# Attention measured in another order, an expert schedule with earlier lists, and the two arms of a branch swapped

## The chip, the core and the metric

The kernel runs on one core of a Trainium2 chip. A core has five engines with instruction streams of their own: PE (matmul), DVE (vector), ACT (scalar and activation functions), POOL (general, and here the issuer of gathers and scatters), and SP (issues plain DMAs). They work in parallel and wait for one another on semaphores. Data lies in the DRAM of the chip (HBM), in SBUF (128 partitions), and in PSUM (eight banks of 128 by 512 float32 values), into which PE writes. The metric is the time of one execution on the device in microseconds (us); lower is better. A profile is one execution; its span runs from the first instruction to the last, and the time of the execution is a little more.

## The reference

A layer of a Flamingo model: attention from tokens to a context, with a gate, and then a mixture of eight experts with a gate. There are 8 batches of 512 tokens, 256 channels, 16 heads of 16 channels, and all is float32.

```python
x = x + tanh(g_xattn[0]) * xattn(layernorm(x), ctx, ctx, mask, wq, bq, wk, bk, wv, bv, wo, bo)
x = x + tanh(g_ffn[0]) * ffn(layernorm(x), router_w, router_b, expert_up, expert_down)

def xattn(query, key, value, mask, ...):
    q, k, v = query @ wq.T + bq, key @ wk.T + bk, value @ wv.T + bv      # in 16 heads
    scores = einsum('bhqd,bhkd->bhqk', q, k) / sqrt(16)
    scores = where(mask == 0, -1e9, scores)
    return (softmax(scores) @ v) @ wo.T + bo

def ffn(x, ...):
    probs = softmax(x @ router_w + router_b)
    top_w, top_idx = top_k(probs, 2)
    comb = sum(top_w * one_hot(top_idx, 8))
    return sum(comb[:, e] * (gelu(x @ expert_up[e].T) @ expert_down[e].T) for e in range(8))
```

`expert_up[e]` is 1024 by 256 and `expert_down[e]` 256 by 1024. The mask is 1 by 1 by 512 by 512 and the same for all batches and heads; it is 0 for a prefix of the keys and 1 for the rest, so that at most 128 keys, those at the end, are attended.

## The kernel before

**Two arms.** A prologue loads the mask and finds whether the attended keys lie within one window of 128. The answer is `near_i`, which every engine loads into a register (L1519). `tc.If` (L1522) then takes one of two arms: `attend_near`, written for a window of 128 keys, or `attend_anywhere` with the experts behind it, for any mask. With these inputs `attend_near` runs. Both are in the program, about as long as each other; in this kernel `attend_near` stands first, so an engine that starts it goes straight on and one that ends it jumps over the other arm.

**Prologue.** It computes for batch 0 the layernorm, the queries (`q_ps`), and from a window of the context the keys and values (`kv_ps`), then takes the mask's column out of the window by a matmul with `pick` (`k_ps`). `idle_ps` are matmuls without use that keep PE active.

**Layernorms.** `measure` gives three steps: `look` (four pairs of BATCH_NORM_STATS2 and AGGREGATE on DVE, L225 and L228), `settle` (thirteen small DVE operations, L233 to L246, that make the reciprocal root of the variance and the shift), and the scaling (`scale`, L275: four ACT operations, xn = x times rstd plus shift). `turn` then transposes xn on PE (`xnT_ps`) and copies it on ACT (L286). The letter a marks the norm ahead of the attention, f the one ahead of the experts. `settle` of two norms can go together.

**The attention's loop.** For b from -1 to 7 there are four groups g (which half c of the channels and which half i of its heads) of three slots n. In a slot the hand-written part comes first: `weigh` (`n_av`, weights times values) for the group before, `find_tops` (scores `t_ps` on PE, their maximum over keys by `tops` on DVE, L1033) for the group that follows, `lower_tops` (`top_ps`, a transpose, and `ql`, the queries with their maximum). `weights_T` makes the group's scores again with the maximum subtracted (`w_ps`, PE L1058), exponentiates them on ACT (`n_pT`, L1063). `raw`, `inv`, `n_o`, `oT` on DVE divide the weighted sums. Then come the steps that `between` put into `plan[g, n]` for other batches: the projection of the batch just finished (`proj_ps`, with the add `x` on DVE, L1102), its norm f, router logits (`logits`: `route_ps` on PE, `lgT` on ACT), routing (`route`, below), the places of its tokens in the experts' lists (`place`: `place_ps` on PE, `counts` on ACT), their entry into a table in DRAM (`enter`: scatters by POOL, L398), and for coming batches the norm a, `queries`, `keys_values` (`kv_ps`), `keys_T` (`k_ps` and ACT's four copies `k`, L551 and L557) and `keys_less` (`km`).

`route` (L330) transposes the logits into PSUM (`lg_ps`), adds the router's bias (`lg`), and takes softmax and the two largest with their indices on DVE (L338 to L360), with one Exp on ACT (L341).

**Order.** The tile framework schedules instructions and may move them within an engine's stream. `tc.keep_in_program_order(ins)` pins an instruction, that is, those pinned keep their order on the engine. Of each pair of scalings in `scale` only the first is pinned.

**Experts.** The tokens of one expert come in jobs of up to three tiles of 128. 32 jobs (`MAIN`) always run, more only if needed. A job s has the steps `list_rows(s)` (SP reads a register and copies the table's lines of this job into SBUF as `listed`, L806), `fetch(s)` (POOL gathers the tokens' rows into `xg` by `listed`, L826), `load(s)` (SP loads the expert's `up` and `down`, 1 MB each), `turn_rows(s)` (`xT`), `ups` (`h_ps` on PE, Gelu on ACT, L874 and L878), `fetch_y` (POOL gathers the output so far), `downs` (`o_ps` on PE, `y` on DVE, L892 and L895, and POOL's scatter into `out`, L898). The dictionary `amid` puts the first four jobs (`DONE`) into the attention's loop at (b, g). The rest run in `compute`, which lists job s + 4 and loads job s + 2 while it runs job s. A copy from the table waits for the entries made before it in the program. The norm, routing and places of the last two batches are interleaved into these jobs, one step of `queue` after each step of `compute`.

Of the kernel before, what the change touches and what calls it, by code (L numbers as in the profile page):

```python
# [16 lines left out]
ALU = mybir.AluOpType  # L17
AX = mybir.AxisListType
# [50 lines left out]
def flamingo_layer(ctx: ExitStack, tc: tile.TileContext, a: dict, out: bass.AP):  # L69
# [190 lines left out]
    def shared(p2, small, bank):  # L260
        def layernorms(jobs, pin=False, measured=None):


            said, looks, settle_all = measured or measure(small, [job[:2] for job in jobs], pin)
            settle = lambda pin=False: settle_all(pin)

            def own(k):
                b, which, dst = jobs[k]

                def scale(ts):  # L270
                    if ts[0] == 0:
                        said[k] = p2.tile([P, QT, D], F32, tag="xn", name=f"xn_{which}_{b}")
                    for t in ts:
                        at = k * QT + t
                        ins = nc.scalar.activation(  # L275
                            said[k][:, t, :], xs[b][:, t, :], AF.Identity,
                            bias=said["shift"][:, at : at + 1], scale=said["rstd"][:, at : at + 1],
                        )
                        if t == ts[0] and pin:
                            tc.keep_in_program_order(ins)  # L280

                def turn(c):
                    ps = bank(f"xnT_ps_{which}_{b}_{c}")
                    for t in range(QT):
                        nc.tensor.transpose(ps[:, t * P : (t + 1) * P], said[k][:, t, c * P : (c + 1) * P], ident)
                    nc.scalar.copy((dst() if callable(dst) else dst)[:, c, :], ps)  # L286

                return (
                    lambda: said[k], [lambda ts=ts: scale(ts) for ts in ((0, 1), (2, 3))],
                    [lambda c=c: turn(c) for c in range(DC)],  # L290
                )

            return looks, settle, [own(k) for k in range(len(jobs))]
# [7 lines left out]
        def finish(b):  # L301
# [28 lines left out]
            def route():  # L330
                ps = bank(f"lg_ps{b}")[:, :P]
                nc.tensor.transpose(ps, said["lgT"], ident)
                lg = t3("lg")
                nc.vector.tensor_tensor(
                    lg, ps.rearrange("p (t e) -> p t e", t=QT)[:, :, :E], over_t(rb), ALU.add
                )
                mx = t2("mx")
                nc.vector.tensor_reduce(mx, lg, AX.X, ALU.max)  # L338
                nc.vector.tensor_tensor(lg, lg, over_e(mx), ALU.subtract)
# [64 lines left out]
            places = [place] + [lambda t=t: enter(t) for t in range(b * QT, (b + 1) * QT)]  # L404
            return x2T, keep_x, keep_rows, logits, route, places

# [42 lines left out]
    with early, tc.tile_pool(name="ps_mask", bufs=1, space=PSUM) as ps_mask:  # L449
# [23 lines left out]

        norms_0 = measure(const, [(0, "a")], True)
        settle_0 = norms_0[2]
# [39 lines left out]
        win = load_window(mk, 0)  # L515
        load_x(1, pin=True)
        wins = {1: load_window(const, 1, pin=True)}
# [90 lines left out]
        nc.vector.scalar_tensor_tensor(near, uneven, 0.0, near, ALU.is_le, ALU.mult)  # L608
        tc.keep_in_program_order(nc.vector.tensor_copy(near_i, near))
        drop = column("drop", P)  # L610
        tc.keep_in_program_order(nc.vector.tensor_scalar(drop, row_ps, -1.0, 1.0, ALU.mult, ALU.add))
# [8 lines left out]

        keep_ones(vals[0])
        for t in vals[1:]:
            keep_ones(t)
# [5 lines left out]
    def experts(pool, seen, half_bank, bank, row_bank):  # L629
# [283 lines left out]

        def compute(s, end, first):

# [13 lines left out]
            else:  # L929

                steps += up[:2] + last + up[2:]
            if s + 4 < end:
                steps.append(lambda: list_rows(s + 4))
# [34 lines left out]
    def attend_near(att):  # L968
# [136 lines left out]

        def normalize(*jobs):
            looks, settle, each = layernorms(jobs, True)
            for job, own in zip(jobs, each):
                normal[job[:2]] = own
            return looks, settle  # L1110

        def between(old, new, next_):
# [9 lines left out]
            if old is not None:  # L1122
                x2T, keep_x, keep_rows, logits, route, place = finish(old)
                jobs.append((old, "f", x2T))
# [5 lines left out]
            if new is not None:  # L1130
# [4 lines left out]
                if new == 1:  # L1135
                    put(1, 1, *turns)
                    put(2, 1, keys_T)
                    put(3, 1, queries[0])
                    put(3, 2, queries[1], keys_less)
                else:  # L1140
                    put(1, 1, *turns, keys_T)
                    put(3, 0, keys_less)
                    put(2, 0, queries[0])
                    put(2, 1, queries[1])
# [6 lines left out]
            if next_ is not None:  # L1151
                put(*((2, 2) if old is None else (0, 2)), looks[-1])
            if old is not None:
# [4 lines left out]
            if jobs:  # L1158
                put(*((3, 1) if old is None else (1, 2)), settle)
            if old is not None:  # L1160
# [5 lines left out]
                counts = [count for count, end in zip(plans, PARTS) if old + 1 == end]  # L1166
                later.append((route, place, enter, counts))
            return plan


        def begin():
# [21 lines left out]
            (7, 3): [lambda: list_rows(5), lambda: fetch(5)] + downs(3)  # L1193
            + [lambda: load(5), lambda: turn_rows(4), lambda: list_rows(6), lambda: list_rows(7)],
        }
        DONE = 4


        xnT, later = {}, deque()
        looks, settle = normalize((1, "a", lambda: xnT[1]))  # L1200
        for step in (*looks, settle):
            step()
        behind = None
        for b in range(-1, B):
# [10 lines left out]
            if b == 0:  # L1215
                plan[0, 0] += looks
                plan[0, 1].insert(0, settle)
            for route, place, enter, counts in behind_route:
                plan[0, 2].append(route)
                plan[1, 2].append(place)  # L1220
# [26 lines left out]
        wait = lambda: None  # L1247
        (route, place, enter, _), (route_last, last, enter_last, counts) = later
        mixed = [step for pair in zip(rest, [route, place, *enter] + [wait] * len(rest)) for step in pair]
        spread = [step for one in enter_last for step in (one, wait, wait)]  # L1250
        queue = deque([*mixed, route_last, last, *spread, *counts])
        for s in range(DONE, MAIN):
            for step in compute(s, MAIN, DONE):
                step()
# [9 lines left out]
    def attend_anywhere(att):  # L1264
# [143 lines left out]
        def end(b):  # L1408
            x2T, keep_x, keep_rows, logits, route, place = finish(b)
            (look,), settle, ((normal, scales, turns),) = layernorms([(b, "f", x2T)])  # L1410
            return [keep_x, look, settle, *scales, lambda: keep_rows(normal()), *turns, logits, route, *place]

# [108 lines left out]
    )  # L1521
    with tc.If(is_near == 1) as which, ExitStack() as att:  # L1522
        attend_near(att)
    with which.Else():
        with ExitStack() as att:
            attend_anywhere(att)
        with ExitStack() as exp:
# [16 lines left out]
            for s in range(MAIN):  # L1544
                for step in compute(s, MAIN, 0):
                    step()
            compute_extra()


# [41 lines left out]
```

## Time and profile before

| what | value |
| --- | --- |
| median of 6 runs | 813.78 us (812.47 to 815.03) |
| time of the profiled execution | 813.25 us |
| its span | 811.5 us |
| mean granted PE clock | 0.968 of full |
| `h_ps` (L874), 1,024 matmuls | 242.9 us |
| `o_ps` (L892), 1,088 matmuls | 243.4 us |
| POOL's three indirect transfers of the experts (L898, L826 twice) | 199.4 us |
| HBM read, written | 92.66 MB, 20.28 MB |

The two groups of expert matmuls make up 60% of the span. The page cuts the span into 40 slices of about 20.3 us; each digit is a share in tenths:

```
PE   8999988888989989999899999999999999999992
DVE  7876885859674664533163353525343433423300
PEclk9997998989899998999999999999999999999997
DMA  5700211000473230143738566666644754654310
```

The first half is the attention, in which DVE is almost as busy as PE; from slice 21 on the experts are alone. Waits of PE by what they were for, from the summary of waits (total, times, longest):

```
PE o_ps L892 <- DVE y L895: 4.2, 4, 1.2
PE lg_ps L332 <- DVE x L1102: 4.1, 4, 1.7
PE x_ps L849 <- DVE raw L1082: 4.1, 2, 3.6
PE route_ps L323 <- ACT x2T L286: 3.6, 1, 3.6
PE xnT_ps_a L285 <- DVE x L1102: 3.5, 3, 1.2
```

At the end the last scatter into `out` is issued at 797.03 us, POOL waits for its landing until 801.7, and the span ends at 811.5 us with the engines' drains.

### The profile page before, as it was taken

Reading aid. Unit: us, or ns where it says so; the run is one execution under the profiler, and the core shown is the slowest. Engines: PE = TensorE matmul, PEld = TensorE weight load, DVE = VectorE, ACT = ScalarE, POOL = GpSimd, SP = SyncE. Lnnn points to the kernel's source line nnn. Section 1 sums busy time; section 2 is a strip of 40 time slices with the busy share of each in tenths; the row PEclk is TensorE's granted clock in tenths of the full one; section 3 lists DMA queues with packets and bytes.
Section 4 is the critical chain, followed back from the end, with each engine's and each line's share of the span. In section 5 each row is a group of like instructions: output and inputs, shape, how many; then the busy total and the mean of one; then the engine's idle time right before and its main releaser. Section 6 shows DMA issues by size and latency. Waiting matters only on the chain. (4 is left out here: it accounts for less than half of the span.)

```text
span 811.5 us, 11155 instructions
## 1 busy us (share of the span) xinstructions
PE 754.4 (93%) x3898; PEld 542.4 (67%) x3898; DVE 409.7 (50%) x1315; ACT 254.7 (31%) x487; POOL 311.5 (38%) x420
## 2 busy tenths in 40 slices
PE   8999988888989989999899999999999999999992
PEld 3444443434465746767688888888788788888871
DVE  7876885859674664533163353525343433423300
ACT  4564745354544434243312111111211211121110
POOL 2021115152637261536563534444443443334330
PEclk9997998989899998999999999999999999999997
DMA  5700211000473230143738566666644754654310
GB/s 163 265 7 8 78 34 56 27 30 27 164 284 116 93 114 20 54 152 106 242 117 308 188 225 205 207 221 201 234 162 152 240 180 153 200 213 163 98 53 24
DMA packets 82728, 113.32 MB, mean 140 GB/s; under 512 B 16605, under 2 KB 67552, under 8 KB 82656
## 3 DMA queue, kind: packets, MB, share of 16 engines
q1 hardware_dynamic: 70000, 85.16, 31.3%
q0 software_dynamic: 11840, 26.76, 10.0%
q8 instruction: 35, 0.57, 0.3%
q10 hardware_dynamic: 816, 0.53, 0.2%
q14 instruction: 37, 0.30, 0.1%
HBM read 92.66 MB, written 20.28 MB: 139 GB/s over the span
## 5 line engine op out<-in xcount | busy, mean ns | idle before, releaser
L892 PE MATMUL o_ps<-down,hT 128*128 128x256 f32 x1088 | 243.4, 381 | 4.2 <-DVE y L895 4.2
L874 PE MATMUL h_ps<-xT,up 128*128 128x256 f32 (+1 forms) x1024 | 242.9, 393 | 3.4 <-DVE xT L851 2.0
L892 PEld LDWEIGHTS o_ps<-down,hT 128*128 128x128 f32 x1088 | 206.1, 191 | 40.5 <-DVE y L895 6.0
L874 PEld LDWEIGHTS h_ps<-xT,up 128*128 128x128 f32 x1024 | 193.2, 190 | 46.4 <-issue 5.4
L863 DVE STREAM_TRANSPOSE xT<-xg 32x128 f32<-32x128 f32 (+1 forms) x368 | 115.7, 314 | 179.7 <-DMA xg<-rows,listed 175.0
L878 ACT ACTIVATE hT<-h_ps 128x512 f32<-128x512 f32 (+1 forms) x144 | 82.1, 573 | 345.8 <-PE h_ps L874 308.7
L898 POOL DMA_INDIRECT out<-y,listed x68 | 68.4, 1006 | 148.4 <-DVE y L895 127.6
L826 POOL DMA_INDIRECT y<-out,listed x68 | 64.9, 955 | 77.1 <-DMA out<-y,listed 48.0
L1033 DVE TENSOR_REDUCE tops<-t_ps 128x4 f32<-128x512 f32 x128 | 79.5, 681 | 24.2 <-PE t_ps L1028 17.5
L1063 ACT ACTIVATE n_pT<-w_ps 128x512 f32<-128x512 f32 x128 | 67.8, 597 | 49.5 <-PE w_ps L1058 45.0
L826 POOL DMA_INDIRECT xg<-rows,listed x68 | 66.1, 972 | 37.6 <-issue 18.9
L398 POOL DMA_INDIRECT table<-entries,place_i x64 | 62.8, 981 | 25.3 <-issue 16.5
L895 DVE SCALAR_TENSOR_TENSOR y<-o_ps,listed,y 128x256 f32<-128x256 f32 x68 | 31.2, 481 | 74.7 <-PE o_ps L892 51.4
L1058 PE MATMUL w_ps<-ql,km 32*128 32x512 f32 x256 | 54.3, 695 | 1.8 <-DVE tops L1033 1.5
L1010 POOL TENSOR_TENSOR x<-x,bo 128x1024 f32<-128x1024 f32 x8 | 18.8, 2354 | 73.1 <-DVE bo L1009 42.3
L1028 PE MATMUL t_ps<-k,q 32*128 32x256 f32 x512 | 44.9, 423 | 1.3 <-ACT n_pT L1063 0.9
L1082 DVE STREAM_TRANSPOSE raw<-n_av 128x512 f32<-128x512 f32 x32 | 22.8, 712 | 42.7 <-PE n_av L1076 23.1
L1028 PEld LDWEIGHTS t_ps<-k,q 32*128 32x128 f32 x512 | 27.6, 194 | 22.8 <-issue 9.7
L1076 PE MATMUL n_av<-n_pT,nv 128*32 128x512 f32 x256 | 38.1, 670 | 1.2 <-DVE xT L851 1.1
L570 PE MATMUL q_ps<-n_xnT,wqT 128*128 128x512 f32 x64 | 31.4, 615 | 0.9 <-ACT n_xnT L286 0.6
L1097 PE MATMUL proj_ps<-woT,oT 128*128 128x256 f32 x128 | 31.5, 388 | 0.0
L1097 PEld LDWEIGHTS proj_ps<-woT,oT 128*128 128x128 f32 x128 | 23.4, 190 | 8.8 <-DVE mv_f_a L228 2.5
(220 smaller groups left out, 529.9 us busy)
## 6 DMA issues: line engine op xcount, KB each, us to landing
up<-in_upT SPq DMA_DIRECT2D x32, 1024.0 KB
down<-in_downT SPq DMA_DIRECT2D x32, 1024.0 KB
out<-x SPq DMA_DIRECT2D x8, 512.0 KB
rows<-xn_f SPq DMA_DIRECT2D x8, 512.0 KB
x<-in_x SPq DMA_DIRECT2D x7, 512.0 KB
table<-none SPq DMA_DIRECT2D x1, 2400.0 KB
xg<-rows,listed POOLq DMA_INDIRECT x68
y<-out,listed POOLq DMA_INDIRECT x68
```

The lines of the kernel that those rows point to most:

```text
L398: nc.gpsimd.indirect_dma_start(out=table_parts[2 * t + i][:, :], out_offset=bass.IndirectOffsetOnAxis(ap=place_i[:, t, i : i + 1], axis=0) ...
L826: ins = nc.gpsimd.indirect_dma_start(out=dst, out_offset=None, in_=src[: seen[JOBS[s][0]], :], in_offset=bass.IndirectOffsetOnAxis(ap=list ...
L863: nc.vector.transpose(dst[32 * g : 32 * g + 32, i], src[32 * i : 32 * i + 32, g])
L874: nc.tensor.matmul(ps[:, i, :], lhsT=up[:, dc, (f + i) * P : (f + i + 1) * P], rhs=xT[:, dc, :], start=(dc == 0), stop=(dc == DC - 1),)
L878: nc.scalar.activation(made[s][:, f : f + m, :], ps, AF.Gelu)
L892: nc.tensor.matmul(ps, lhsT=hT[:, f, h * P : (h + 1) * P], rhs=down[:, f, :], start=(f == 0), stop=(f == FC - 1))
L898: ins = nc.gpsimd.indirect_dma_start(out=out_parts[h][:, :], out_offset=bass.IndirectOffsetOnAxis(ap=listed[:, n, h, 0:1], axis=0), in_=y[ ...
L1028: ins = nc.tensor.matmul(ps[j][:, u], lhsT=q[rows_j, c, t * P : (t + 1) * P], rhs=k[rows_j, c], start=True, stop=True)
L1033: nc.vector.tensor_reduce(top[:, 2 * tp : 2 * tp + 2, :].rearrange("p t (i x) -> p t i x", i=2)[:, :, :, 32 * j], ps[j], AX.X, ALU.max,)
L1058: ins = nc.tensor.matmul(ps[j], lhsT=km[rows_j, c, i, :], rhs=lowered[b, c][rows_j, i, :], start=True, stop=True)
L1063: nc.scalar.activation(pT[:, j, :], ps[j], AF.Exp)
L1097: nc.tensor.matmul(ps[:, t - ts[0], :], lhsT=outs[b, c][:, t * P : (t + 1) * P], rhs=w["woT"][:, c, :], start=(c == 0), stop=(c == DC - 1),)
```

## The change

It has these parts:

1. In `scale` all four ACT operations are pinned.
2. `route` is cut in two. `route` now only transposes and adds the bias, and stands at (0, 0) of the next batch's plan. `choose` does the rest and stands at (0, 2), where all of it stood; its first DVE operation is pinned.
3. Batch 1's x is loaded ahead of batch 0's window on SP, and its `look` and `settle` run in the prologue on DVE, ahead of the branch, into tiles of the constant pool; inside `attend_near` they are gone.
4. In the pass b = 0, in which no older batch is to be finished, batch 3's `look` goes from (2, 2) to (1, 2) and its `settle` from (3, 1) to (2, 0).
5. `keys_T` goes from (1, 1) to (1, 2). There it stands directly ahead of the `place` of the finished batch, with which it shares a PSUM bank.
6. Jobs 6 to 16 (up to `LISTED`) are all listed in one step at (7, 3); `compute` lists from job 17 on.
7. The arms are swapped: `attend_anywhere` is first in the program, `attend_near` last. An engine now jumps over the other arm as it starts `attend_near`, and has nothing to jump over at its end.
8. In the tail's queue `route` and `choose` of one batch are one step.

```diff
@@ def scale
-                        if t == ts[0] and pin:
+                        if pin:
                             tc.keep_in_program_order(ins)
@@ def finish
             def route():
                 ps = bank(f"lg_ps{b}")[:, :P]
                 nc.tensor.transpose(ps, said["lgT"], ident)
-                lg = t3("lg")
+                said["lg"] = t3("lg")
                 nc.vector.tensor_tensor(
-                    lg, ps.rearrange("p (t e) -> p t e", t=QT)[:, :, :E], over_t(rb), ALU.add
+                    said["lg"], ps.rearrange("p (t e) -> p t e", t=QT)[:, :, :E], over_t(rb), ALU.add
                 )
+
+            def choose():
+                lg = said["lg"]
                 mx = t2("mx")
-                nc.vector.tensor_reduce(mx, lg, AX.X, ALU.max)
+                tc.keep_in_program_order(nc.vector.tensor_reduce(mx, lg, AX.X, ALU.max))
...
@@ prologue
-        norms_0 = measure(const, [(0, "a")], True)
+        load_x(1, pin=True)
+        norms_0, norms_1 = (measure(const, [(b, "a")], True) for b in range(2))
...
         win = load_window(mk, 0)
-        load_x(1, pin=True)
...
         tc.keep_in_program_order(nc.vector.tensor_copy(near_i, near))
+        norms_1[1][0]()
...
         keep_ones(vals[0])
+        norms_1[2](True)
@@ def compute
-            if s + 4 < end:
+            if listed <= s + 4 < end:
                 steps.append(lambda: list_rows(s + 4))
@@ def between
-                    put(1, 1, *turns, keys_T)
+                    put(1, 1, *turns)
+                    put(1, 2, keys_T)
...
-                put(*((2, 2) if old is None else (0, 2)), looks[-1])
+                put(*((1, 2) if old is None else (0, 2)), looks[-1])
...
-                put(*((3, 1) if old is None else (1, 2)), settle)
+                put(*((2, 0) if old is None else (1, 2)), settle)
@@ amid
-            + [lambda: load(5), lambda: turn_rows(4), lambda: list_rows(6), lambda: list_rows(7)],
+            + [lambda: load(5), lambda: turn_rows(4), lambda: [list_rows(s) for s in range(6, LISTED)]],
         }
         DONE = 4
+        LISTED = SIZES[0] + SIZES[1]
@@ the attention's loop
-            for route, place, enter, counts in behind_route:
-                plan[0, 2].append(route)
+            for route, choose, place, enter, counts in behind_route:
+                plan[0, 0].append(route)
+                plan[0, 2].append(choose)
                 plan[1, 2].append(place)
@@ the tail's queue
+        def choice(route, choose):
+            route()
+            choose()
+
+        first = [lambda: choice(route, choose), place, *enter]
+        mixed = [step for pair in zip(rest, first + [wait] * len(rest)) for step in pair]
...
-        queue = deque([*mixed, route_last, last, *spread, *counts])
+        queue = deque([*mixed, lambda: choice(route_last, choose_last), last, *spread, *counts])
@@ the branch
-    with tc.If(is_near == 1) as which, ExitStack() as att:
-        attend_near(att)
-    with which.Else():
+
+    with tc.If(is_near == 0) as which:
         with ExitStack() as att:
             attend_anywhere(att)
...
+    with which.Else(), ExitStack() as att:
+        attend_near(att)
```

## The prediction

> **What bounds the kernel now.** I read the page first, then windows by stage, then the timelines of the stages that stood out. The page:
>
> ```profile
> span 811.5 us, 11155 instructions
> ...
> PE 754.4 (93%) x3898; PEld 542.4 (67%) x3898; DVE 409.7 (50%) x1315; ACT 254.7 (31%) x487; POOL 311.5 (38%) x420
> ...
> L1033 DVE TENSOR_REDUCE tops<-t_ps 128x4 f32<-128x512 f32 x128 | 79.5, 681 | 24.2 <-PE t_ps L1028 17.5
> ```
>
> PE (the matmul engine) is busy 93% of the span, so only its idle time and the time that it runs at half clock can be won. The windows say where they are (columns: stretch, length, each engine's busy time and count, granted clock, DMA share, GB/s):
>
> ```profile
> 60.00:76.00 16.00, 14.54 (x62) 6.57 (x62) 9.84 (x30) 7.02 (x15) 2.34 (x1) 0.68 0.03 10
> 100.00:210.00 110.00, 92.94 (x592) 45.08 (x588) 83.30 (x270) 56.55 (x120) 36.76 (x69) 0.93 0.12 37
> 430.00:797.00 367.00, 362.07 (x1609) 304.92 (x1607) 135.75 (x407) 62.25 (x110) 153.51 (x157) 1.00 0.56 187
> ```
>
> From 430 us on the experts run at full clock with 5 us idle: nothing to win. In 100 to 210 PE idles 17 us and loses clock; in 60 to 76 the clock is 0.68. PE there:
>
> ```profile
> 62.35 1.12 PE L1058 MATMUL w_ps<-ql,km 32*128 32x512 f32 x2
> 64.93 3.26 PE L1058 MATMUL w_ps<-ql,km 32*128 32x512 f32 x6 [1.46 <-DVE tops L1033]
> 68.12 1.93 PE L1076 MATMUL n_av<-n_pT,nv 128*32 128x512 f32 x8
> 69.99 3.78 PE L539 MATMUL kv_ps<-wkv,win 128*128 128x512 f32 x4
> 73.70 1.38 PE L1028 MATMUL t_ps<-k,q 32*128 32x256 f32 x16
> ```
>
> Six w_ps take 3.26 us where eight take 1.14 at 108.33; kv_ps takes 3.78 where 1.98 is usual (38.38). PE stopped for tops, and the clock halved. Tops was late because DVE measured batch 3 (st_a at 58.71 to shift_a, raw at 62.75: 4.04 us) with t_ps already done at 61.84.
>
> **The change, part by part.** The sum is made against the profiled run's own 813.25 us (811.5 span, 1.75 around it); the median of six, 813.78, lies 0.53 above it, which I add at the end.
>
> *Batch 3 measured sooner.* The 4.04 us move to before raw at 52.66. DVE idles 1.35 there and 0.69 at 54.9, so 2.04 are covered and 2.0 delay tops and w_ps of that group. In return the stall at 62.35 falls away: at the usual paces w_ps, n_av, kv_ps, t_ps take 1.07 + 1.0 + 1.9 + 1.1 and end at 67.4 instead of 75.08, 7.6 sooner. 7.6 − 2.0 = **−5.6**. Other bound: if the displaced 2.0 us stop PE and halve its clock for one spell of 6.83 us (3.4 lost), 5.4 of 5.6 are given back: 0. I take −5.6, since 2.0 us is less idle than what halved the clock at 131 to 134 (below).
>
> *Batch 1 measured in the prologue.* Its loads are issued on SP ahead of the window's, some 7 us sooner. Its look falls into a DVE idle of 1.51 us at 15.8; its settle (2.5 us) comes after the first keep_ones. DVE thus reaches the branch near 21.1 instead of 18.3, while at present the settle stands behind the branch and holds the first tops to 24.23. Same work in another place: 0 apart from the jump. The earlier load is 512 KB, 1.4 us at the 365 GB/s of that stretch; on SP it now stands ahead of the two window loads, the gates and the small constants, but the DMA engines are idle from 9.8 to 14, so it is off the queue before the windows are issued (12.87): 0, at worst +1.4 if it slows the mask, whose last quarter DVE reads at 8.7.
>
> *The arms swapped.* At the start each engine now takes a jump over the other arm, and at the end none. What a taken jump costs shows at the end of the present program:
>
> ```profile
> L1522 PEldq COMPARE_BRANCH  x1: 90/90/90, 20.1 to 20.1; - x1
> ...
> L959 PEldq COMPARE_BRANCH  x2: 3821/4201/4581, 793.0 to 797.2; - x2
> ...
> L1587 POOLq DRAIN  x3: 40/107/4734, 806.0 to 811.3; - x3
> ...
> L1587 DVEq DRAIN  x2: 10/38/65, 802.1 to 811.0; - x2
> ```
>
> Not taken 0.09 us, taken 3.8 to 4.6 on PE. POOL, last at the end, branches at 803.22 and drains from 805.96: 2.74 us on the path, then 4.73 of drain. **−2.7**; bounded by 0 if the drain ends by something else. At the start PE branches at 20.12; with 4.2 its first t_ps comes at 24.3 instead of 21.83, the first tops about 24.7. DVE took 4.3 from its branch (797.83) to its drain (802.13): from 21.1 that is 25.4. ACT, 2.4 by its own end, reaches its scalings (24.40) 0.4 late. DVE is the bound from 24.23 to 35.85 (four rounds of tops, each 2.48), so its own delay is what counts: 0.5 to 1.2, taken **+1.1**; upper bound +3.5, if PE's 2.5 us of waiting halves its clock.
>
> The Trainium skill bears on this with two places that disagree. Advanced Engine Details and Errata, Control Flow Timing, gives a compare-and-branch about 108 ns; the row of 3,821 to 4,581 ns is some forty times that, so by the page both jumps would be worth an estimated 0.1 us and the sum would lose both terms. Runtime: NRT & Kernel Launch, Instruction fetch mechanics, says that a taken branch out of the fetched window must wait for a new page; that fits the row, and speaks against this change, as the wait is only moved to the start.
>
> *Route split, scalings pinned, keys_T later.* In each of five passes (b = 2 to 6; here b = 2) PE waits thus:
>
> ```profile
> 108.07 0.33 PE L332 MATMUL lg_ps<-ident,lgT 128*128 128x128 f32 x1 [0.80 <-DVE x L1102]
> 115.23 0.66 PE L285 MATMUL xnT_ps_a<-ident,xn_a 128*128 128x128 f32 x4 [1.18 <-DVE x L1102]
> 118.06 0.38 PE L368 MATMUL place_ps<-both,before 128*128 128x32 f32 x2 [0.84 <-ACT k L557]
> ```
>
> lg_ps moves two slots ahead, where its bank is free: −0.8. place_ps now stands directly behind k_ps in one PSUM bank and waits for ACT's four copies of k (1.51 us): about +0.85, with w_ps and n_av queued behind it. But DVE is busy without a break from 104.93 to 124.55, and its x add still releases xnT_ps_a, so PE gains nothing by coming sooner, and most of place's wait fits into the slack ahead of the next tops. Pinned scalings take three ACT operations of 0.52 from ahead of n_pT to another place, worth the 0.45 that t_ps waits at 123.72. I take **0** for the passes; bounds five times −0.8 and +0.85: −4.0 to +4.3.
>
> *Lists 6 to 16 at (7, 3), queue of the tail.* Today a list waits on SP for table entries of batches 6 and 7 that it does not read, and the loads behind it wait too. In 360 to 430:
>
> ```profile
> L874 PE MATMUL h_ps<-xT,up 128*128 128x256 f32 x152 | 35.2, 383 | 3.4 <-DVE xT L851 2.0 <-DMA up<-in_upT 1.4
> ```
>
> All 3.4 is the upper gain, 0 the lower: nine more lists then stand ahead of load 6 on SP, 3 KB each, while PE has other jobs. I take **−2.0**: the wait for up, and a third of that for xT. Route and choose of batches 6 and 7 in one step reorder PE work that the experts' matmuls surround: 0. Where choose's Exp falls between Gelus in batches 6 and 7, ACT reloads its table (1,283 ns each, L878 and L341 there); ACT is idle 34.5 us ahead of its Gelus in that stretch, which hides it, and uncovered it would be 1.3 to 2.6.
>
> Sum: +1.1 − 5.6 + 0 − 2.0 − 2.7 = −9.2. 813.25 − 9.2 = 804.05, and with 0.53 the median: **804.6**.
>
> **The rivals.** *Slower: place_ps halves the clock in each pass.* At 131.37 and 133.02 PE idled 1.22 + 1.70 = 2.92 us within 3.4, and the clock halved at 135.67 for 6.83 us. At 114 to 118 it idled 1.18 + 0.23 + 0.84 = 2.25 and the clock held. With 0.85 more that is 3.1: past the mark, if it lies close enough. Price per pass 0.85 + 3.4 = 4.25. From three of five passes on the rest is outweighed: 12.75 − 9.2 = +3.55, **817.3**; with all five 825. For it: the two idles above, and three spells (135, 173, 207) already within 110 us. Against: the three waits stretch over 4.6 us, and DVE sets the pass, so PE slack absorbs the 0.85.
>
> The page TensorE: Matmul & The Clock Gate, Part 1, has the clock judged in free-running windows of about 3.4 us and only full or half; the spells here, 6.83 and 10.24 us long, are whole multiples of 3.41 and agree. By it 3.1 us over 4.6 would not always fill a window.
>
> *The stall only moves.* Batch 3's measuring stops PE at 55 instead (0 for that term), the start costs 2.5, lists hide nothing, the end gives 2.7: 813.25 − 0.2 + 0.53 = **813.6**. For it: DVE had only 2.04 idle there. Against: tops at 55.60 would be late by 2.0, not by 4.
>
> *Part of the change does not do what it says.* The drain of POOL ends when it did, and the lists were not what held up and xT: −2.7 and −2.0 are lost, 804.6 + 4.7 = **809.3**.
>
> **How the numbers follow.** Forecast 0.50, partial effect 0.16, moved stall 0.12, slower by the clock 0.22. 0.2% is 1.6 us, about what a measurement of this kernel can tell from no change. The moved stall gives 0.03 to faster, 0.06 to same and 0.03 to slower: faster 0.69, same 0.06, slower 0.25. The forecast's own range is 800 to 808 (half of the passes' −4.0, and the start's +3.5 or a lesser gain at 60). For 8 in 10 I go from 799 to 816: it takes in the partial and the moved case, and leaves out most of the slower one.
>
> **What would show it.** Right: w_ps, n_av and kv_ps near 60 to 68 at 1.1, 1.0 and 2.0 us and a clock of 1.00 there; PE's first t_ps near 24.3; POOL's drain straight behind its semaphore work, with no 2.7 between; h_ps in the stretch from 360 to 430 with under 1.5 us of waits; place_ps waiting 1.7 on k, with tops no later. Wrong: clock spells at place_ps, a spell at 55, first tops past 27, or a spell of DVE and ACT lateness such as the 4.04 us at 134.93 in new places, for which this trace shows no cause.

## The result, and the profile after

The changed kernel takes 816.38 us (median of 41 runs), the kernel before 813.41 us (83 runs): a ratio of 1.0025, interval 1.0015 to 1.0035. By the ratio it is slower by about 2 us (the medians lie 3.0 apart); 804.6, with a range to 816, was predicted. The profiled execution took 815.19 us with a span of 813.4. The windows of the changed kernel, in the stretches shown of before (columns as there: stretch, length, busy time and count of PE, PEld, DVE, ACT, POOL, granted clock, DMA share, GB/s):

```profile
60.00:76.00 16.00, 16.00 (x100) 7.43 (x100) 13.12 (x25) 8.60 (x18) 4.46 (x2) 1.00 0.03 10
100.00:210.00 110.00, 92.62 (x594) 47.09 (x596) 81.98 (x270) 55.62 (x116) 37.19 (x70) 0.89 0.10 32
210.00:430.00 220.00, 195.48 (x1128) 141.17 (x1120) 105.74 (x380) 87.30 (x152) 104.62 (x161) 0.95 0.43 141
430.00:797.00 367.00, 361.33 (x1604) 303.98 (x1604) 138.55 (x416) 63.44 (x112) 153.99 (x158) 1.00 0.55 184
```

At 60 to 76 the stall is gone and the clock stays full, as forecast. From 100 to 430 PE idles more than before. When the same matmul starts in the two profiles, read from the two timelines, shows where the time comes and goes:

| point | before, us | after, us | difference | change of it |
| --- | --- | --- | --- | --- |
| first `w_ps` | 37.31 | 40.52 | +3.2 | +3.2 |
| sixth group of `w_ps` | 77.37 | 74.45 | -2.9 | -6.1 |
| last group of `w_ps` | 343.21 | 343.20 | 0.0 | +2.9 |
| 193rd `h_ps` | 388.65 | 385.82 | -2.8 | -2.8 |
| 289th `h_ps` | 438.63 | 444.27 | +5.6 | +8.5 |
| 993rd `h_ps` | 768.48 | 775.17 | +6.7 | +1.1 |
| end of the span | 811.54 | 813.42 | +1.9 | -4.8 |

The 193rd, 289th and 993rd `h_ps` are the first of jobs 6, 9 and 31. The +3.2 at the first `w_ps` is more than one effect: with the arms in their old order (a run below) the changed kernel has it at 36.47, so the swapped arms cost 4.0 there, and the other parts, batch 1 in the prologue first of all, give 0.8 back.

The start, from the instructions of the branch's line and PE's timeline of the changed kernel (in the first line: durations in ns, first and last start):

```profile
L1535 PEldq COMPARE_BRANCH  x1: 4197/4197/4197, 19.9 to 19.9; - x1
```

```profile
24.25 1.94 PE L1033 MATMUL t_ps<-k,q 32*128 32x256 f32 x16 [2.99 <-issue]
26.12 2.84 PE L542 MATMUL kv_ps<-wkv,win 128*128 128x512 f32 x4
```

PE jumps for 4.2 us, idles 2.99 of them, and then runs at half clock: kv_ps takes 2.84 instead of 1.98. The stall near 62 has gone and kv_ps and t_ps have their usual lengths; only the eight w_ps ahead of them take 2.97, where 1.1 was expected:

```profile
65.20 2.97 PE L1063 MATMUL w_ps<-ql,km 32*128 32x512 f32 x8
...
69.10 1.98 PE L542 MATMUL kv_ps<-wkv,win 128*128 128x512 f32 x4
71.02 1.15 PE L1033 MATMUL t_ps<-k,q 32*128 32x256 f32 x16
```

The first pass, PE's timeline after:

```profile
111.93 0.66 PE L285 MATMUL xnT_ps_a<-ident,xn_a 128*128 128x128 f32 x4 [1.82 <-DVE x L1107]
...
116.17 0.60 PE L371 MATMUL place_ps<-both,before 128*128 128x32 f32 x2 [1.69 <-ACT k L560]
```

lg_ps no longer waits, but xnT_ps_a waits 0.64 more for the same x add, and place_ps 0.85 more for k. The clock halves there in the first two of three passes, which it did not before. Windows of 8 us around this place, after and then before (granted clock third from the end):

```profile
113.00:121.00 8.00, 6.07 (x26) 2.87 (x26) 5.87 (x25) 3.62 (x10) 2.62 (x13) 0.57 0.17 61
154.00:162.00 8.00, 6.17 (x25) 2.87 (x26) 5.94 (x25) 3.68 (x10) 2.71 (x13) 0.57 0.17 61
194.00:202.00 8.00, 6.40 (x45) 2.85 (x44) 6.86 (x40) 5.18 (x12) 3.85 (x14) 1.00 0.09 30
```

```profile
116.00:124.00 8.00, 6.48 (x41) 2.80 (x44) 7.49 (x28) 4.62 (x11) 3.48 (x14) 1.00 0.19 66
156.00:164.00 8.00, 6.55 (x44) 2.93 (x44) 7.49 (x28) 4.67 (x12) 3.89 (x15) 1.00 0.20 65
```

The 8.5 us between the 193rd and the 289th h_ps are the largest loss. That stretch before, and after:

```profile
388.65:438.63 49.98, 45.11 (x227) 38.28 (x226) 17.25 (x86) 11.30 (x19) 28.34 (x40) 1.00 0.59 197
```

```profile
385.82:444.27 58.45, 48.10 (x228) 40.42 (x226) 17.33 (x86) 11.39 (x19) 32.11 (x44) 0.88 0.41 144
```

PE idles 5.5 us more, and for the same matmuls it is busy 3.0 us longer, at a clock of 0.88. PE's timeline after, and DVE's and ACT's:

```profile
397.82 0.48 PE L332 MATMUL lg_ps<-ident,lgT 128*128 128x128 f32 x1 [3.72 <-ACT lgT L328]
...
405.18 5.74 PE L879 MATMUL h_ps<-xT,up 128*128 128x256 f32 x14 [6.04 <-DVE lg L342]
```

```profile
403.89 0.19 DVE L334 TENSOR_TENSOR lg<-lg_ps,rb 128x32 f32<-128x32 f32 x1 [17.82 <-remote]
```

```profile
397.50 0.27 ACT L328 COPY lgT<-route_ps 128x128 f32<-128x128 f32 x1 [6.99 <-remote]
402.45 0.60 ACT L883 ACTIVATE hT<-h_ps 128x512 f32<-128x512 f32 x1 [4.69 <-remote]
```

lg waits for lg_ps alone. PE's record of lg_ps ends at 398.3, and DVE, idle, starts lg at 403.89. ACT, idle, starts lgT at 397.50, though route_ps ended at 390.45. "remote" says that no instruction in the profile ended when the wait did. I call this a late start. POOL at that time, after and then before:

```profile
382.61 1.07 POOL L401 DMA_INDIRECT table<-entries,place_i  x1 [0.92 <-DMA up<-in_upT]
383.99 0.97 POOL L401 DMA_INDIRECT table<-entries,place_i  x1 [0.31 <-issue]
...
392.83 1.00 POOL L831 DMA_INDIRECT xg<-rows,listed  x1 [0.30 <-DMA table<-entries,place_i]
...
399.25 1.01 POOL L903 DMA_INDIRECT out<-y,listed  x1 [0.30 <-issue]
402.51 0.99 POOL L831 DMA_INDIRECT y<-out,listed  x1 [2.25 <-DMA out<-y,listed]
```

```profile
379.00 0.97 POOL L398 DMA_INDIRECT table<-entries,place_i  x1 [0.30 <-issue]
383.16 0.96 POOL L398 DMA_INDIRECT table<-entries,place_i  x1 [3.20 <-DMA listed<-table]
...
393.31 1.03 POOL L898 DMA_INDIRECT out<-y,listed  x1 [0.30 <-issue]
396.27 0.97 POOL L826 DMA_INDIRECT xg<-rows,listed  x1 [1.93 <-remote]
```

Before, POOL's scatters waited 3.20 us for a list's copy out of the table, and 9 indirect transfers followed without a break. After, no list is in the way, and 14 follow one another at 1.26 us each, from 382.6 to 400.3; the last of these late starts ends 3.6 us behind it. In the trace of before all five late starts over 1.5 us (DVE at 134.93, 174.31 and 302.60, ACT at 173.98 and 396.03) end 1.5 to 1.8 us behind an unbroken run of eight or nine. Two of them:

```profile
134.93 2.48 DVE L1033 TENSOR_REDUCE tops<-t_ps 128x4 f32<-128x512 f32 x4 [4.04 <-remote]
```

```profile
396.03 0.27 ACT L328 COPY lgT<-route_ps 128x128 f32<-128x128 f32 x1 [5.72 <-remote]
```

The reverse does not hold: of the eight runs of eight or nine in that trace four have no late start behind them. That such runs make starts late is what the experiments had to test.

At the end the last scatter is issued at 803.72 instead of 797.03, but the span ends 9.7 us behind it instead of 14.5:

```profile
L1600 POOLq DRAIN  x3: 40/107/4652, 807.9 to 813.1; - x3
...
L964 POOLq EVENT_SEMAPHORE  x5: 17/43/1864, 804.3 to 806.5; - x5
```

POOL's drain follows its semaphore work directly, without the jump of 2.74. A further 1.6 us come from the wait for the last landing, 1.86 instead of 3.49.

### The profile page after: what moved, and what is told of

It is laid out like the page before. It is cut to its first block, busy times and chain, and to the rows that moved or that the text cites. A ratio compares the mean times of both kernels' runs of the same rounds, so it can differ in the third digit from the quotient of the medians.

```text
span 813.4 us, 11126 instructions
## 1 busy us (share of the span) xinstructions
PE 748.6 (92%) x3898; PEld 543.1 (67%) x3898; DVE 409.0 (50%) x1315; ACT 261.9 (32%) x491; POOL 312.4 (38%) x420
## 5 line engine op out<-in xcount | busy, mean ns | idle before, releaser
L1033 PE MATMUL t_ps<-k,q 32*128 32x256 f32 x512 | 41.3, 425 | 3.0 <-issue 3.0
L1033 PEld LDWEIGHTS t_ps<-k,q 32*128 32x128 f32 x512 | 25.8, 195 | 19.7 <-issue 14.4
L1081 PE MATMUL n_av<-n_pT,nv 128*32 128x512 f32 x256 | 35.8, 633 | 2.9 <-DVE xT L856 2.8
```

What stands on the lines that cost most here:

```text
L1033: ins = nc.tensor.matmul(ps[j][:, u], lhsT=q[rows_j, c, t * P : (t + 1) * P], rhs=k[rows_j, c], start=True, stop=True)
```

## The experiments

The chips differ, so ratios are to the kernel before on the same chip. On chips 7, 5 and 11 it took 813.4 to 815.7 us, on chips 14 and 1 it took 792.4 to 792.7.

**Lists as before (chip 7).**

```diff
-            ... lambda: [list_rows(s) for s in range(6, LISTED)]],
+            ... lambda: list_rows(6), lambda: list_rows(7)],
-            for step in compute(s, MAIN, DONE, LISTED):
+            for step in compute(s, MAIN, DONE):
```

> The changed kernel with the lists as before: job s+4 is listed while job s runs, 6 and 7 at (7, 3). Theory L: with all lists there early, nothing stops POOL between the table scatters of batch 6 and the gathers of the jobs, its run of indirect transfers grows, and PE's signals reach ACT and DVE only after its end; that costs the 8.3 us that PE lost between 388 and 425 us. So this kernel takes about 808 us (816.4 less 8.3), with the waits of lg_ps and h_ps near 394 to 405 down from 3.7 and 6.0 us to 2.5 and 1. Theory C: the loss comes from choose, pinned and with its Exp between two Gelus; then the time stays at 816 and the two waits stay.

813.37 us, 0.9989 (0.9964 to 1.0013): 0.36% under the changed kernel's 1.0025, less than half of what I expected. Between the 193rd and the 289th h_ps it loses 1.0 against before instead of 8.5, with lg_ps waiting for nothing, but it loses 3.85 just ahead of that, where h_ps waits for up. So the lists are part of it, and something else costs as well.

**The kernel before with the lists early and nothing else (chip 7).** The opposite edit.

> The kernel before with nothing but lists 6 to 16 in one step at (7, 3). Theory L: about 820 us (813.4 plus 6 to 8), with the long waits of PE for lgT and lg near 395 to 405. Theory C, and my prediction's own step: 811 to 813.4, a gain of 0 to 2 us.

819.07 us, 1.0053 (1.0033 to 1.0074): 4.3 us slower. POOL's run is 14 again, lg_ps waits 5.78 and h_ps 1.97. My own step had the sign wrong here, and choose and the pins are not needed for the loss.

**Arms as before (chip 7).** The changed kernel with `attend_near` first again.

> The changed kernel with the arms in their old order. If the swap moves a wait from the end to the start and no more, the start is 2.4 to 3.2 us sooner (first t_ps near 21.6) and the end 4.8 later (scatter to end of span 14.5 instead of 9.7): net 1.6 to 2.4 slower, about 818. Rival: the start's delay is swallowed by later slack, so the swap is worth the whole 4.8: 821. Other rival: the 2 us by which the last landing was shorter in the changed kernel is chance, so the end's gain is 2.7 and the net 0: 816.

819.06 us, 1.0072 (1.0041 to 1.0102): the swap is worth 0.47%, 3.8 us. Its interval, 1.2 to 6.4, takes in both the expected 1.6 to 2.4 and the rival's 4.8; it excludes only that the swap is worth nothing.

**Batch 3 sooner alone (chip 7).**

```diff
-                put(*((2, 2) if old is None else (0, 2)), looks[-1])
+                put(*((1, 2) if old is None else (0, 2)), looks[-1])
-                put(*((3, 1) if old is None else (1, 2)), settle)
+                put(*((2, 0) if old is None else (1, 2)), settle)
```

> The kernel before with batch 3's look at (1, 2) and settle at (2, 0), nothing else. If the 5.8 us won near 60 to 75 stay to the end: about 807.6. Rival: the passes after it give part of it back (in the changed kernel PE was 2.9 us ahead of before at 100 and 0.3 ahead at 175), so 811 to 812.

810.5 us, 0.9959 (0.994 to 0.9977): 3.3 us. In its profile PE is 4.8 ahead at the sixth w_ps and 5.4 at the last; 3.5 are left at the end. From the first to the sixth w_ps batch 3 alone wins 5.0 of the 6.1.

**Lists and keys_T as before (chip 5).**

```diff
-                    put(1, 1, *turns)
-                    put(1, 2, keys_T)
+                    put(1, 1, *turns, keys_T)
```

> The changed kernel with the lists and also keys_T as before, so that k_ps no longer stands directly ahead of place_ps. From 95 to 200 us PE lost 2.6 to 3.3 us against the kernel before in all three kernels that had the split route, the pinned scalings and the later keys_T, and won 0.9 in the one with batch 3 alone. Theory K: the later keys_T is the cause (waits of place_ps 1.66 instead of 0.84, and of xnT_ps_a 1.8 instead of 1.2); then this kernel is 3 to 4 us faster than with the lists alone undone, about 0.994 of the kernel before. Theory P: the split route or the pinned scalings cause it; then it stays at 0.9989 within 0.002.

806.22 us, 0.9899 (0.9875 to 0.9922). Against 0.9989 with the lists alone undone, the later keys_T costs 0.9%, some 7 us (5 to 10, and the two runs are from two chips). PE's waits of place_ps for k are 1.7 us in all instead of 4.9 (three waits each). The rest fits late starts: with the later keys_T those of one batch ran into a scatter of y, nine in a row up to 260.7, and DVE's raw was 6.4 late behind them; without, eight up to 255.8 and nothing late. That is one trace of each, so this share is not shown.

**Enter steps spread over more slots, with batch 3 sooner (chip 5).** The four enter steps at (1, 2), (2, 1), (3, 0), (3, 2).

> The kernel before with batch 3 measured sooner, and the four enter steps (two table scatters each) at (1, 2), (2, 1), (3, 0) and (3, 2) instead of four slots in a row. Theory S: ACT and DVE get PE's signals late while POOL issues eight or more indirect transfers without a break, until 1.5 to 3.6 us after the last. With the runs broken up, the late starts at 128 and 168 (gaps of 2.2 to 5 us on ACT and DVE) and the waits of route_ps there (2.63 + 1.03 and 3.70) go, 3 to 8 us faster than batch 3 alone, 803 to 808 beside 810.5. Rival: the waits come from something else in that stage (DMA traffic, the order on ACT); then they stay, at the same matmuls, and the time is 810 to 812.

807.96 us, 0.995 (0.9922 to 0.9978), no different from batch 3 alone. It tells nothing: in the trace POOL still issued eight scatters in a row, since they wait for nothing that the slots contain.

**Batch 3 and the arms; and batch 1 too (chip 5).** The parts that won, on the kernel before.

> The kernel before with batch 3 measured sooner and the arms swapped, nothing else. If the swap is worth the 3.8 us that it was worth in the changed kernel: 810.5 - 3.8 = 806.7 (ratio 0.991 against 0.9959 for batch 3 alone). Rival: without batch 1 in the prologue DVE's settle still stands behind the jump, the start is 3 to 4 us late, and only 1 is left: 809.5.

> As the one with batch 3 and the arms, and batch 1 measured in the prologue too. If DVE's settle behind the jump costs, this is 1 to 2.5 us faster than without batch 1; if PE's jump and the half clock after it set the start, the two are the same within 1 us.

808.13 us, 0.9928 (0.9905 to 0.9952), and 805.72 us, 0.9909 (0.9885 to 0.9933). The swap is worth 0.3% here; batch 1 in the prologue adds 0.2%, inside the intervals. The second of these and the changed kernel without lists and keys_T (0.9899) lie together, so the split route and the pinned scalings move nothing that these runs can tell.

**Pauses on POOL (chip 14).** Ahead of each pair of scatters, on the kernel with the lists early and on the one with batch 3, arms and batch 1:

```diff
+    pause = fixed([P, 4], "pause", I32)
...
+                    if i == 0:
+                        for _ in range(6):
+                            tc.keep_in_program_order(nc.gpsimd.memset(pause, 0))
-                    nc.gpsimd.indirect_dma_start(
+                    ins = nc.gpsimd.indirect_dma_start(
...
+                    tc.keep_in_program_order(ins)
```

> The kernel before with lists 6 to 16 early, and six small memsets on POOL ahead of each pair of table scatters, so that a run of indirect transfers is broken after every second one; POOL does nothing else in them. Theory S (PE's signals reach ACT and DVE late while POOL issues eight or more indirect transfers without a break): the long waits of lg_ps and h_ps near 395 to 405 (5.8 and 2.0 us with the lists alone) and the late starts of ACT and DVE there shrink below 2 us in all, and the passes gain too: 4 to 10 us faster than the lists alone, ratio 0.993 to 1.000 instead of 1.0053. Rival: the early lists cost by the order of the steps or by what the copies do on the queue; then pauses change nothing or cost, 1.005 to 1.008.

> Batch 3 sooner, arms swapped, batch 1 in the prologue (0.9909 of before), with the same pauses. Theory S: the waits of route_ps near 130, 170 and 208 (1.2 to 3.7 us each, with half clock after some) and of x_ps near 297 (3.5) go: 4 to 10 us less, ratio 0.979 to 0.986. Rival: they stay, ratio 0.990 to 0.993.

810.96 us, 1.0234 (1.0212 to 1.0255), and 806.47 us, 1.0161 (1.014 to 1.0182). Neither theory had said that. The kernel before took 792.72 us on this chip, and none of the four traces from it has a late start over 1.2 us, with or without pauses.

**keys_T later alone; scalings unpinned (chip 14).**

> The kernel before with nothing but keys_T at (1, 2). If it costs what it cost in the changed kernel without early lists (0.9989 against 0.9899, 7 us): 1.006 to 1.010. If it costs only the added wait of place_ps, 0.85 us in four or five passes: 1.004 to 1.005. My prediction's own step: 0 to 0.2%, swallowed by DVE.

> The changed kernel with lists and keys_T as before (0.9899), and the scalings pinned as before, only the first of each pair. If the pins do nothing: 0.988 to 0.992. If they help, 0.993 or more; if they cost, 0.987 or less.

795.78 us, 1.004 (1.0025 to 1.0055): 3.2 us. The trace shows the added wait, 1.69, 1.60 and 1.60 of place_ps in three passes instead of 0.84, 0.75 and 0.75, and no late start. It also shows half clock at each of the three. Windows of 6 us at each place_ps, and the same of the kernel before with early lists (a run below, on chip 1), where keys_T is as it was:

```profile
117.00:123.00 6.00, 5.53 (x23) 2.05 (x24) 5.32 (x22) 3.63 (x9) 3.06 (x14) 0.72 0.00 0
151.00:157.00 6.00, 4.67 (x21) 1.43 (x22) 4.97 (x23) 3.51 (x9) 2.79 (x13) 0.72 0.03 8
186.00:192.00 6.00, 4.84 (x22) 1.85 (x23) 4.67 (x27) 2.41 (x7) 2.74 (x13) 0.72 0.05 17
```

```profile
117.00:123.00 6.00, 5.32 (x34) 2.08 (x34) 5.52 (x24) 2.62 (x7) 3.30 (x14) 1.00 0.00 0
150.00:156.00 6.00, 5.25 (x30) 1.97 (x30) 5.55 (x24) 2.66 (x7) 3.24 (x14) 1.00 0.07 24
183.00:189.00 6.00, 5.25 (x32) 2.13 (x34) 5.34 (x28) 2.89 (x8) 2.80 (x13) 1.00 0.23 78
```

From the first place_ps to that of the next pass the one takes 34.86 us and the other 33.44.

Unpinned: 788.17 us, 0.9939 (0.9916 to 0.9962). The same kernel with pins ran only on chip 5, so this can't be read as an effect of the pins.

**The same again on one chip without late starts (chip 1).**

> The kernel before with lists 6 to 16 early, once more. The last four kernels ran on a chip on which the kernel before takes 792.7 us instead of 813 to 815 and on which no start of ACT or DVE is late behind a run of POOL's transfers. Theory S: on such a chip the early lists cost nothing, ratio 0.996 to 1.001, with waits for lgT and lg near 390 under 1 us; on a chip with the late starts they cost again, 1.003 to 1.008. Rival: their cost is in the order of the steps and the queue, then it is 1.003 to 1.008 on any chip.

> The same with pauses on POOL ahead of each pair of scatters. Theory S: on a chip with late starts it is faster than the lists alone by 4 to 10 us, and its time is that of the other chip, 809 to 813; on a chip without them it is slower than the lists alone by 15 to 20 us, as the pauses then only make POOL late. Rival: the same difference on any chip.

> The changed kernel, once more, beside the others on one chip. Theory S: on a chip without late starts it keeps its gains (batch 3, arms, batch 1: together 8) and pays only the added wait of place_ps (3 us): ratio 0.990 to 0.996. On a chip with late starts 1.002 to 1.004. Rival: 1.002 to 1.004 on any chip.

> Batch 3 sooner, arms swapped, batch 1 in the prologue, once more. All three win where no late start bears on them (before 100 us and at the end), so 0.989 to 0.993 on any chip. Rival: part of the gain came from the late starts falling otherwise; then 0.995 or more on a chip without them.

| kernel | chip with late starts | chip without |
| --- | --- | --- |
| before with early lists | 1.0053 (1.0033 to 1.0074) | 0.9975 (0.9956 to 0.9995) |
| the changed kernel | 1.0025 (1.0015 to 1.0035) | 0.9951 (0.9929 to 0.9973) |
| batch 3, arms, batch 1 | 0.9909 (0.9885 to 0.9933) | 0.9917 (0.9896 to 0.9938) |
| early lists with pauses | 0.9947 (0.993 to 0.9965), the run below | 1.0162 (1.0119 to 1.0206) |

Here the early lists win 2 us and the whole change 3.9. What wins without POOL wins the same on both. PE and POOL of the changed kernel on this chip, the place shown above:

```profile
371.08 0.27 PE L332 MATMUL lg_ps<-ident,lgT 128*128 128x128 f32 x1
371.19 0.60 PE L854 MATMUL x_ps<-ident,xg 128*128 128x128 f32 x4
372.68 3.29 PE L879 MATMUL h_ps<-xT,up 128*128 128x256 f32 x14 [0.89 <-DVE xT L856]
```

```profile
361.86 1.07 POOL L401 DMA_INDIRECT table<-entries,place_i  x1 [0.92 <-DMA up<-in_upT]
...
378.48 1.01 POOL L903 DMA_INDIRECT out<-y,listed  x1 [0.30 <-issue]
```

POOL's run is the same 14, from 361.9 to 379.5; lg_ps, in the middle of it, waits for nothing, and h_ps 0.89 instead of 6.04.

**Early lists with pauses on a chip with late starts (chip 11).**

> Early lists with pauses on POOL, once more, for a chip with late starts. On the chip without them the pauses cost 15 us (1.0162 against 0.9975), mostly as gathers of the first jobs came later (6.2, 5.1 and 6.0 us waits). Theory S, on a chip with late starts: no start of ACT or DVE late by more than 1.2 us behind the scatters of the passes, PE's waits of route_ps at 130 and 170 under 1 us each; the time is that of the other chip, 803 to 814, so 0.988 to 1.000 of the kernel before. If pauses do not help there, the late starts stay and the time is 1.0053 + 0.018, some 833 us.

811.68 us, 0.9947 (0.993 to 0.9965), where the lists without pauses had 1.0053 on chip 7. That chip 11 is of the same kind rests on its time of the kernel before, 815.71. The windows:

```profile
100.00:210.00 110.00, 97.01 (x671) 49.71 (x671) 92.53 (x287) 59.18 (x127) 49.95 (x148) 0.98 0.17 53
210.00:430.00 220.00, 204.57 (x1109) 148.87 (x1110) 103.70 (x374) 77.22 (x139) 117.40 (x280) 0.95 0.44 143
```

In 100 to 210 PE runs 671 matmuls instead of the 583 of the lists without pauses, at a clock of 0.98 instead of 0.91, much as the changed kernel does on chip 1 (680, 0.97). No late start over 0.6 us is left in the passes. The time is close to that of the other chips, 806 to 811: with the runs broken the chips differ by 1 to 6 us instead of 21. What the pauses win in the passes they lose with the jobs, whose gathers come later (o_ps waits 4.69 and 4.88 near 420 and 440).

**Pauses only for batches 0, 1, 3 and 4 (chip 5),** on batch 3, arms and batch 1.

> Batch 3 sooner, arms swapped, batch 1 in the prologue, lists, route, scalings and keys_T as in the kernel before, and the pauses on POOL only for the scatters of batches 0, 1, 3 and 4, behind which no job's gather waits. On a chip with late starts theory S gives 0.9909 less the waits at 130, 170 and 298 (3 to 4 us each with the clock): 0.978 to 0.984. If the pauses only cost, 0.991 to 1.000. On a chip without late starts 0.990 to 0.996.

801.68 us, 0.9851 (0.9818 to 0.9884): a little less gain than I expected, but the fastest kernel on such a chip, faster than both the kernel before and the changed one. The one trace holds both cases. DVE in batch 0, with the run broken, and in batch 2, with eight scatters in a row until 198.36:

```profile
127.46 0.72 DVE L1090 STREAM_TRANSPOSE raw<-n_av 128x512 f32<-128x512 f32 x1 [1.37 <-PE n_av L1084]
...
129.49 2.49 DVE L1041 TENSOR_REDUCE tops<-t_ps 128x4 f32<-128x512 f32 x4 [0.49 <-PE t_ps L1036]
```

```profile
199.84 0.72 DVE L1090 STREAM_TRANSPOSE raw<-n_av 128x512 f32<-128x512 f32 x1 [4.86 <-remote]
```

One late start stands behind a broken run too (ACT at 298.04, 1.97 us).

## Why the prediction was wrong

**Lists: the step that failed.** "I take −2.0", between 0 and −3.4. The waits that it counted did go: by the 161st h_ps the kernel with early lists alone is 2.9 us ahead. But the waits were also what broke POOL's run. I had seen the late starts and named them at the end as having no cause in the trace; what I missed is that all of them stood behind a run of eight or nine, and that the lists would make one of 14. A spell of such lateness in new places was among the signs of being wrong, and it came. Measured: +4.3 us on a chip with late starts, −2.0 (−3.5 to −0.4) on one without.

**Passes: the other step that failed.** "I take 0", on the ground that DVE sets the pass and PE's slack absorbs the 0.85. The forecast waits came (place_ps 0.85 more, xnT_ps_a longer by most of what lg_ps won), but in three passes and not in the five that were counted: in the trace of before, too, place_ps waits for k only three times. They were not swallowed: the later keys_T alone costs 3.2 us (2.0 to 4.4), and the added waits are 2.55.

My slower rival had this place and this mechanism, and the first of the signs of being wrong came: with keys_T alone the clock halves at all three place_ps (0.72 over 6 us is 3.4 us at half), in the changed kernel at two of them, there already behind the longer wait of xnT_ps_a (half from 113.2 and 154.2 on). Its price of 4.25 per pass was too high: the pass grew by 1.4, and 0.85 of that is the wait. That the other 0.55 are the half clock is not shown. On the chips with late starts the later keys_T costs some 7. The clock alone does not rank these kernels: in 100 to 210 it was 0.89 after and 0.93 before, but also 0.88 in the kernel that had keys_T and the lists undone and was 10 us faster in the median. It has spells in the same place, from 152.1 and 193.0 on, so in the changed kernel the split route can bring them too.

**Batch 3.** Forecast −5.6; in the profiles −6.1 from the first to the sixth w_ps, full clock at 60 to 76; batch 3 alone gives −5.0. The mechanism was right. In the time only 3.3 arrive, as later stages give part of it back.

**The arms.** At the start +1.1 was taken, with DVE as the bound. PE was the bound, by its jump of 4.2, of which it idles 2.99, and the half clock (0.57 at 24 to 28) after it; DVE waited 2.06 and 1.36 us for its t_ps. The swap costs 4.0 at the first w_ps, over the upper bound of 3.5. Batch 1, taken as 0, gives 0.8 back there (40.19 with it, 40.99 without, in the pair on the kernel before), which leaves +3.2. Not all of the 4.0 stays: by the last w_ps it is 1.2, with late starts in between. At the end −2.7 was taken and −4.8 came, the jump as forecast and the rest from the last landing. Net 2.5 and 3.8 us were won in the two pairs (0 to 5 and 1.2 to 6.4), where −1.6 was the sum of the two terms: both were off, in opposite ways, so that the sum is near is luck in part. By the Trainium skill's Advanced Engine Details and Errata, Control Flow Timing, a compare-and-branch takes about 108 ns; the row at the start says 4,197, and the row decides.

**Why it summed to a loss.** By ratios on the chips with late starts: batch 3, arms and batch 1 −0.9%, lists +0.36 to +0.53%, keys_T +0.9%, in all +0.36 to +0.53%, which the measured +0.25% fits within the intervals. All gains that I forecast for them exist; two terms that I took as a small gain and as nothing were a loss as large as they. On chip 1, without late starts, taken group by group, only the passes fail: batch 3, arms and batch 1 were forecast at −7.2 and give −6.6, the lists at −2.0 and give −2.0. With the +3.2 of keys_T from chip 14 that makes −5.4, where −3.9 (−5.6 to −2.1) was measured.

**What stays open.** That unbroken runs of POOL's transfers make the starts late is shown by the pauses (lists with pauses against lists without, and broken beside unbroken runs in one trace). Why only some of these runs do it is not, and eight is no threshold: in the run with the arms as before DVE starts 6.12 us late at 371.18 behind a run of six. What on the way is held up is not shown either. PE's matmul ends are modelled, so the traces can't say if the signal or PE's last write is late. That the two kinds of chip differ by the late starts alone is argued from the times with broken runs. Nor is it known what in the chips differs. Whether the pins or the split route have a small effect was not separated.

## What to carry to other kernels

A wait that bounds nothing can still hold apart what must not run together: before taking one away, look at what its engine will then do without a break, and at what has been late behind such stretches. Waits that the profile puts down to nothing it can name belong in the first reading, since their common neighbour (here an unbroken run of POOL's transfers) is a cause to be tested. And a change of 0.3% has to be timed on more than one chip: this one is 0.25% slower on one kind and 0.5% faster on a chip of the other.

## What was not expected of the hardware

- The five chips fall into two kinds for this kernel, 813 to 816 us and 792 us for the same program, 2.6%. The late starts go with most of the difference: with POOL's runs broken one kernel takes 812 on the one kind and 806 to 811 on the other.
- Late starts reached 17.8 us of idle DVE while POOL kept its beat of 1.26 us per transfer. The Trainium skill's page SBUF — State Buffer, Who interferes with whom, has DVE and POOL share a pair of ports as an exclusive lock, in which whichever issues first blocks the other, and says that PE and ACT never wait on anyone. Here ACT was late too (6.99 us), so that rule alone does not cover it.
- A taken jump over the other arm costs PE 4.2 us at the start (after) and 4.6 at the end (before), one over the jobs that are not needed 3.3 and 3.8. At the start half clock follows (0.57 at 24 to 28).
